# Layer 3's two sets of scans in one sequence with weights set up beside the end of layer 2, images moved in thirds, and GpSimd side steps in the sixth group

## The chip, the core and the metric

The program runs on one core of a Trainium2 chip, as one launch. Its engines work side by side and meet at semaphores: TensorE (PE), VectorE (DVE), ScalarE (ACT), GpSimd (POOL) and SyncE (SP, which here only issues DMA transfers). The metric is the time on the device from the first to the last instruction, in microseconds; lower is better.

## The reference

Four images of 48 x 48 positions with 192 channels pass through four layers, all in fp32. The core of each is a selective scan with 16 states a channel, over the 2,304 positions of an image or over each of its 48 rows or columns:

```python
def step(h, t):                      # one position of a sequence
    d_t, u_t, b_t, c_t = t
    h = exp(d_t[..., None] * A) * h + (d_t * u_t)[..., None] * b_t[:, None, :]
    return h, sum(h * c_t[:, None, :], -1)
# layer 0: _mamba = in_proj, causal conv, silu, scan, gate silu(z), out_proj
xw = _mamba(columns) + _mamba(columns reversed)
xh = layernorm(xw as rows) + x;  x = _mamba(xh) + _mamba(xh reversed)
# layer 1: convolutions on half of the channels; on the other half
yv = the scan in 4 directions (rows, columns, both reversed), added up
x = shuffle(concat(conv half, out_proj(layernorm(yv) * silu(z)))) + x
# layer 2: the scan in 4 directions once more, added up
x = layernorm(y)
# layer 3
xn = layernorm(x)
h = _mamba of each row of xn, forward and reversed, concatenated    # set "mh"
v = _mamba of each column of xn, forward and reversed, concatenated # set "mv"
x = x + fc(concat(v, h)) + fc_b
x = x + mlp(layernorm(x))
```

Row-order and column-order versions of the images are both kept in DRAM, since a scan reads its sequence in order.

## The kernel before

**Stages.** Layer 0 is two calls of `mamba_pair`. `vss_inputs` does the convolutions of layer 1. `scan_layers` does the scans of layers 1 and 2 for all four images in one sequence. Layer 3 is `row_mambas` twice, first for the set "mv" on the column-order images `xn_wh`, then for "mh" on `xn_hw`; then `mlp`.

**Jobs and groups.** A *job* is a chunk of 384 positions (6 to an image) in one direction. `run_jobs` runs a list of jobs group by group. A *group* covers 128 partitions of channels and four of the states: VectorE multiplies `du` by the broadcast row B (`inputs`, line 56), scans (`h`), GpSimd multiplies h by the broadcast row C (`h<-h,bcb`), TensorE adds up over the states (`y`), and ACT computes the four exponentials `a` two groups ahead. A job has 6 groups in layers 1 and 2 and 12 in layer 3. The work that prepares the next job (`units`: loads of `u` or `xs`, projections, the convolution, the products for B, C and delta) and that ends the last one (`outputs`) is spread over the groups, at numbered *slots*; slot 0 is a job's first group. What VectorE, GpSimd, TensorE in most of its products, and ACT issue is kept in program order (class `InOrder`, line 48). DMA transfers of SP aren't: they are issued when their inputs and buffers are ready.

**The ends of layers 1 and 2.** When the fourth direction of an image has been scanned, the sum of its directions is normalised and projected, in six chunks of 384 columns, last first. `vss_end` and `ss2d_end` give a list of *steps* for a chunk, each with a kind: "dma" (loads), "act", "pe" (a product into PSUM and its copy by ACT), "both", "pool" (the norm's scale, `nx<-nx,nrs` on GpSimd). `Side` (line 689) puts at most one step into each group, in the slots of the step's kind. What is left after the last scan, which is part of the third image of layer 2 and the fourth image whole, is done by `Side.finish`, with new buffers and all of PSUM.

**Images in column order.** For each image the end of a layer needs the sum of the column directions in row order and gives its result in both orders. At the first chunk (`c == NCH - 1`), `load` loads a whole image, 1.7 MB, into `turned`; each chunk's `turn` copies its part of it (`no<-turned`), and later its results are copied back into the same place (`turned<-no`); after the last chunk (`c == 0`), `turned` is stored whole as `x_wh` or `xn_wh`.

**Layer 3.** `row_mambas` opens its pools, loads the set's weights, multiplies the output projection by the matching part of fc (`fp`), builds its `ScanPools`, and runs its 48 jobs. The second call does so again after the first has run empty. The results f of both sets stay in DRAM apart. `mlp` loads its weights, then at each image's start (`pre`) the residual x3 and both results, adds them up in `macc` by four VectorE passes, one half of the channels each, and goes on chunk by chunk: norm, first product, Gelu, second product.

Of the kernel before, what the change touches and what calls it, by code (L numbers as in the profile page):

```python
# [291 lines left out]


# [395 lines left out]
class Side:  # L689
# [4 lines left out]
    slots = {"pe": (0, 4, 5), "both": (0, 4), "act": (0, 4, 5), "pool": (0, 2, 4), "dma": range(6)}  # L694
# [25 lines left out]
    def finish(self):  # L720

        while self.waiting:
            n = len(self.waiting) if self.waiting[0][0][0] == "dma" else 1
            some, self.waiting = self.waiting[:n], self.waiting[n:]
            for steps in zip(*some):
                for step in steps:
                    self.begin(*step)
                    self.end()


def run_jobs(jobs, side=None):
# [14 lines left out]
    def offer(job):  # L746
        if side is not None and job.steps is not None:
            side.waiting.append(job.steps())
# [12 lines left out]
    for t in range(len(groups) + gated):  # L761
        n, at = divmod(t, per)
        if at == 0:
            last = jobs[n - 1] if n else None
            if n + 1 < len(jobs):
                jobs[n + 1].load()
                stream = Stream(jobs[n + 1].units(last))
        if at == per - ahead:
            stream.run(at - 1)
        if at == taken + 3 and n + 1 == len(jobs) and n:  # L770
            Stream(jobs[n - 1].outputs(*[(0, 0)] * 4)).run(per)
        if t < len(groups):
            job, i, g = groups[t]
            job.scan(i, g)
        coming = at_group(t + 1, 0)
        if t + ahead < len(groups):
            job, i, g = groups[t + ahead]
            job.decay(i, g, (lambda: coming[0].enter(coming[1])) if coming else None)
        if done := at_group(t - taken, last_group):
            done[0].take(done[1])  # L780
        if t < len(groups):
            if t + 1 < len(groups):
                job, i, g = groups[t + 1]
                job.carry(i, g)
            job, i, g = groups[t]
            job.weigh(i, g)
        stream.run(at if at < per - 1 else per)
        if side is not None and t < len(groups):
            if at == taken + 1 and n:
                offer(jobs[n - 1])  # L790
            side.slot(at)
            side.end()
        if done := at_group(t - gated, last_group):
            done[0].gate(done[1])
        if begun := at_group(t + driven, 0):
            begun[0].drive(begun[1])
        if 0 <= t - behind < len(groups):
            job, i, g = groups[t - behind]
            job.reduce(i, g)
# [38 lines left out]
class MambaWeights(Weights):  # L838
    def __init__(self, k, pool, inT, xpT, dtT, vec, tag):
        super().__init__(k, pool, 128, 12, xpT, dtT, vec, tag)  # L840
        self.decays(k)
        nc = k.nc
        self.D = self.vec[:, :, 17:18]
# [7 lines left out]
        self.inT = k.tile(pool, [Q, 2, 768], f"inT{tag}")  # L851
        nc.sync.dma_start(self.inT, inT.rearrange("(k p) m -> p k m", p=Q))
        self.diag = k.tile(pool, [128, 3, self.taps, 128], f"diag{tag}")
        for i in range(3):
            for t in range(self.taps):
                nc.vector.tensor_scalar(
                    self.diag[:, i, t, :],
                    k.ident,
                    self.vec[:, i, 19 + t : 20 + t],
                    None,  # L860
                    ALU.mult,
                )

# [20 lines left out]
def mamba_pair(k, weights, srcs, first, outs, ahead=None):  # L884


    with ExitStack() as ctx:
# [3 lines left out]
        def load():  # L891
            for n, (inT, xpT, dtT, vec, outT) in enumerate(weights):
                w = MambaWeights(k, pool, inT, xpT, dtT, vec, f"_{n}")
                w.outT = k.tile(pool, [128, 3, C], f"outT_{n}")
# [239 lines left out]
class Normed:  # L1134
# [17 lines left out]

    def tile(self, shape, tag, bufs=None):
# [7 lines left out]
    def rows(self, turned, c):  # L1161

        t = self.tile([Q, 2, CH], "no")
        for m in range(2):
            self.k.copy(
                t[:, m, :].rearrange("p (r l) -> p r l", l=S), rows_of(turned[:, m, :], c)
# [49 lines left out]

def rows_of(img, c):
# [28 lines left out]
def scan_layers(k, pool, layers, ends):  # L1246
# [3 lines left out]
    with ExitStack() as ctx:  # L1250
        one = ctx.enter_context(k.tc.tile_pool(name="s1", bufs=1))
        two = ctx.enter_context(k.tc.tile_pool(name="s2", bufs=2))
# [33 lines left out]
        scans.close()  # L1286
        normed.two = ctx.enter_context(k.tc.tile_pool(name="s3", bufs=NCH))
        side.psum = ctx.enter_context(k.tc.tile_pool(name="sp", bufs=8, space=PSUM))
# [3 lines left out]
def vss_end(k, vec, outT, x1, xl, zs, out_hw, out_wh):  # L1292
# [3 lines left out]
    def begin(normed, one):  # L1296
# [5 lines left out]
        turned = {}  # L1302

        def steps(b, c, h_sum, w_sum):
# [3 lines left out]
            def load():  # L1308
                if c == NCH - 1:
                    turned[b] = k.tile(normed.one, [Q, 2, L], "turned")  # L1310
                    nc.sync.dma_start(turned[b], halves(w_sum))
# [8 lines left out]
            def turn():  # L1320
                st["w"] = normed.rows(turned[b], c)
# [14 lines left out]
            def result(s):  # L1336
# [6 lines left out]
                def act(ps):  # L1343
# [3 lines left out]
                    k.copy(rows_of(turned[b][:, s, :], c), ps.rearrange("p (r l) -> p r l", l=S))  # L1347
                    if s == 1:
                        parts = "(c s) l -> c s l"
                        nc.sync.dma_start(out_hw[b].rearrange(parts, s=2)[:, :, at], st["o"])  # L1350
                        if c == 0:
                            nc.sync.dma_start(out_wh[b].rearrange(parts, s=2), turned[b])
# [3 lines left out]
            return [  # L1356
# [6 lines left out]
            ]  # L1363

# [5 lines left out]
def ss2d_end(k, vec, ln1, x3, xn_hw, xn_wh):  # L1370
# [3 lines left out]
    def begin(normed, one):  # L1374
# [4 lines left out]
        turned = {}  # L1379

        def steps(b, c, h_sum, w_sum):
# [3 lines left out]
            def load():  # L1385
                if c == NCH - 1:
                    turned[b] = k.tile(normed.one, [Q, 2, L], "turned")
                    nc.sync.dma_start(turned[b], halves(w_sum))
                st["y"] = normed.load("ny", halves(h_sum)[:, :, at])

            def turn():
                st["w"] = normed.rows(turned[b], c)
# [10 lines left out]
            def second(x, of):  # L1403
                o = normed.tile([Q, 2, CH], "no")
                for m in range(2):
                    of(o[:, m, :], m)
                    k.copy(
                        rows_of(turned[b][:, m, :], c),
                        o[:, m, :].rearrange("p (r l) -> p r l", l=S),
                    )  # L1410
                nc.sync.dma_start(halves(xn_hw[b])[:, :, at], o)
                if c == 0:
                    nc.sync.dma_start(halves(xn_wh[b]), turned[b])

            return [
# [6 lines left out]
            ]  # L1422

# [5 lines left out]
def row_mambas(k, weights, fcT, srcs, outs):  # L1429


    with ExitStack() as ctx:
        pool = ctx.enter_context(k.tc.tile_pool(name="w", bufs=1))
        inT, xpT, dtT, vec, wout = weights
        w = MambaWeights(k, pool, inT, xpT, dtT, vec, "")
        ws = [w, copy(w)]
        wo = k.tile(pool, [Q, 2, 2 * C], "wo")
        k.nc.sync.dma_start(wo, wout.rearrange("(k p) m -> p k m", p=Q))
        fc = k.tile(pool, [Q, 2, 2, C], "fc")
        for n in range(2):  # L1440
            k.nc.sync.dma_start(fc[:, n, :, :], fcT[n].rearrange("(k p) m -> p k m", p=Q))

        outT = [k.tile(pool, [128, 3, C], f"outT_{n}") for n in range(2)]
        with k.tc.tile_pool(name="fp", bufs=2, space=PSUM) as fp:
            for n in range(2):
                for i in range(3):
                    p = k.tile(fp, [128, C], "fp")
                    k.mm(p, [(wo[:, m, i * 128 : (i + 1) * 128], fc[:, n, m, :]) for m in range(2)])
                    k.copy(outT[n][:, i, :], p)
        pools = ScanPools(k, ctx, 1, True)  # L1450
        jobs = []
        for n in range(2):
            ws[n].outT = outT[n]
        for b in range(B):
            for c in range(NCH):
                of = None, srcs[b], outs[b]
                first = MambaJob(k, pools, ws[0], c * CH, False, *of)
                jobs += [first, MambaJob(k, pools, ws[1], c * CH, True, *of, twin=first)]
# [3 lines left out]
def mlp(k, f, fcb, ln2, w1T, b1, w2T, b2, x3, out):  # L1462
# [5 lines left out]
    with (  # L1468
# [5 lines left out]
    ):  # L1474
        w1 = k.tile(one, [Q, 2, 3 * C], "mw1")
# [9 lines left out]
        nw = k.tile(one, [Q, 2, 3], "mnw")  # L1485
        nc.sync.dma_start(nw[:, :, 0:2], ln2.rearrange("(k p) v -> p k v", p=Q))
        nc.sync.dma_start(nw[:, :, 2:3], fcb.rearrange("(k p v) -> p k v", p=Q, v=1))
        acc, xn, hid = {}, {}, {}

        def pre(b):  # L1490
            acc[b] = k.tile(pool, [Q, 2, L], "macc")
            nc.sync.dma_start(acc[b], halves(x3[b]))
            y = []
            for n in (1, 0):
                y.append(k.tile(one, [Q, 2, L], f"mf{n}"))
                nc.sync.dma_start(y[-1], halves(f[n][b]))
            for m in range(2):
                nc.vector.scalar_tensor_tensor(
                    acc[b][:, m, :], acc[b][:, m, :], nw[:, m, 2:3], y[0][:, m, :], ALU.add, ALU.add
                )  # L1500
            for m in range(2):
                nc.vector.tensor_tensor(
                    square(acc[b][:, m, :]),
                    square(acc[b][:, m, :]),
                    flipped(y[1][:, m, :]),
                    ALU.add,
                )
# [33 lines left out]
def network(tc, d, out):  # L1541
    with ExitStack() as ctx:
# [23 lines left out]

        xl, zs = images("xl", Q), images("zs")
# [4 lines left out]
        with tc.tile_pool(name="w", bufs=1) as pool:  # L1572
            weights = []

            def beside(b):
# [19 lines left out]
                ],  # L1595
            )
# [3 lines left out]
        for n, (p, src) in enumerate((("mv", xn[1]), ("mh", xn[0]))):  # L1600
            ws = tuple(d[f"L3_{p}_{v}"] for v in ("inT", "xpT", "dtT", "vec", "Wout"))
            fcT = [d["L3_fcT"][2 * n + i] for i in range(2)]
            row_mambas(k, ws, fcT, src, f[n])
        mlp(k, f, *(d[f"L3_{v}"] for v in ("fc_b", "ln2", "w1T", "b1", "w2T", "b2")), x3, out)


# [115 lines left out]
```

## Time and profile before

| | |
|---|---|
| Median of three runs | 20,027.88 us (20,027.85 to 20,035.81) |
| Profiled execution | 20,028.4 us |
| TensorE, VectorE, GpSimd, ACT busy | 88%, 91%, 73%, 64% |
| Layer 0, first pair and second pair, from first to last scan | 44.5 to 3,131 and 3,331 to 6,419 us |
| `vss_inputs` | 6,422 to 6,925 us |
| `scan_layers`, scans | 6,925.2 to 13,205.4 us (1,152 groups) |
| "mv" and "mh", scans | 13,386.6 to 16,440.0 and 16,503.7 to 19,553.2 us (576 groups each) |
| `mlp` | to 20,028.4 us |

The stages are read from the starts of the scan instruction (`h<-a,inputs`) in the timeline of VectorE. In the profile's list of groups, a line gives the source line, the engine, the operation, output and inputs by the names of the program, their shape, and after x the count; then the total busy time and the mean of one in ns; then the idle time of the engine just ahead of them and what ended most of it. Line 56 is that of the in-order helper and line 93 that of ACT's, so the names tell such operations apart. A line of the waits says which engine and which operation waited for what, then the total time, the number of waits, and the longest. A line of the timeline has start, duration, engine and operation, and in brackets the idle time ahead and its releaser.

### The profile page before, as it was taken

What the parts mean: (1) busy time and instruction counts of PE and PEld (TensorE: products, weight loads), DVE (VectorE), ACT (ScalarE), POOL (GpSimd) and SP (SyncE); (2) the same over time, 40 slices, a digit from 0 to 9 for tenths busy, and PEclk for the clock granted to TensorE, in tenths of its full rate; (3) what the DMA queues carried; (4) which work ended last, traced back from release to release, by engine and by line L of the source; (5) the groups of instructions that cost most, each with busy time, mean ns of one, the idle gap of its engine ahead of it and who ended that gap; (6) DMA issues with size and microseconds to landing.
All of it is one profiled execution on the core that took longest, in us unless ns stands there. A gap on an engine that the chain in (4) does not pass through costs nothing.

```text
span 20028.4 us, 159197 instructions
## 1 busy us (share of the span) xinstructions
PE 17551.3 (88%) x48144; PEld 8281.4 (41%) x48144; DVE 18198.7 (91%) x7435; ACT 12796.7 (64%) x22447; POOL 14681.9 (73%) x10816
## 2 busy tenths in 40 slices
PE   8999997999998878888888888879989989999988
PEld 4444443444444322333333332334444444444444
DVE  8999997999998499999999999969999989999993
ACT  6666665666665466666666766666666656666663
POOL 7888885788786177887877877857777767777770
PEclk9999998999999889999999999989999999999999
DMA  3333333333233366666666666642222222222322
GB/s 116 108 109 110 115 110 111 109 113 115 103 110 100 82 133 138 142 146 146 143 147 143 138 139 144 138 110 103 101 106 104 106 96 106 107 101 102 107 102 59
DMA packets 484426, 2313.40 MB, mean 116 GB/s; under 512 B 75401, under 2 KB 324017, under 8 KB 325553
## 3 DMA queue, kind: packets, MB, share of 16 engines
q1 hardware_dynamic: 483568, 2303.21, 40.7%
q8 instruction: 386, 6.32, 0.1%
q14 instruction: 472, 3.86, 0.1%
HBM read 2110.68 MB, written 192.32 MB: 115 GB/s over the span
## 4 chain that ended last, share of the span: by engine, by line
DVE 35%; POOL 13%; PE 10%; issue 5%; ACT 2%; DMA 2%; DVEq 0%; SPq 0%; POOLq 0%; ACTq 0%
DVE h L56 23%; DVE inputs L56 12%; POOL h L56 10%; PE y L56 5%; PE ps L56 3%; POOL dus L56 1%; PE vps L114 1%; ACT a L93 1%; PE mop L114 1%; PE mps L114 1%; DMA bcb<-bc 1%; POOL state L56 1%; DVE vxi L1056 1%; DVEq L56 0%; POOL bcb L56 0%
## 5 line engine op out<-in xcount | busy, mean ns | idle before, releaser
L56 POOL TENSOR_TENSOR h<-h,bcb 128x1536 f32<-128x1536 f32 x3456 | 11914.0, 3447 | 1764.2 <-DVE h L56 1489.3
L56 DVE TENSOR_TENSOR_SCAN h<-a,inputs 128x1540 f32<-128x1540 f32 (+1 forms) x3456 | 11609.8, 3359 | 449.2 <-ACT a L93 10.8
L93 ACT ACTIVATE a<-delta,A 128x384 f32<-128x384 f32 (+1 forms) x13824 | 7431.8, 602 | 3417.4 <-DVE h L56 3405.2
L56 PE MATMUL y<-h,ident 128*128 128x384 f32 x18432 | 6798.4, 517 | 587.2 <-POOL h L56 581.9
L56 DVE TENSOR_TENSOR inputs<-du,bcb 128x1540 f32<-128x1540 f32 (+1 forms) x3456 | 6115.4, 1770 | 561.0 <-ACT du L93 205.9
L56 PEld LDWEIGHTS y<-h,ident 128*128 128x128 f32 x18432 | 3619.4, 201 | 3625.1 <-POOL h L56 1100.6
L56 PE MATMUL y<-h,sum 128*64 128x384 f32 x9216 | 3666.4, 547 | 598.3 <-POOL h L56 486.6
L56 PEld LDWEIGHTS y<-h,sum 128*64 128x64 f32 x9216 | 1294.8, 150 | 2922.0 <-issue 1755.0
L56 POOL COPY state<-h 128x4 f32<-128x4 f32 x2304 | 434.0, 188 | 2296.2 <-DVE h L56 2277.1
L56 PE MATMUL ps<-xh,diag 128*128 128x384 f32 x4032 | 1417.3, 491 | 196.3 <-ACT xc L93 196.3
L56 PE MATMUL ps<-u,inT 96*128 96x384 f32 x3456 | 1263.1, 497 | 189.9 <-ACT z L93 135.4
L56 PE MATMUL ps<-bcd,dtT 12*128 12x384 f32 (+1 forms) x2304 | 1019.4, 550 | 388.9 <-ACT delta L93 384.7
L56 PEld LDWEIGHTS ps<-xh,diag 128*128 128x128 f32 x4032 | 750.4, 189 | 790.0 <-ACT xc L93 283.0
L93 ACT ACT_TABLE_LOAD x793 | 1017.4, 1283 | 14.2
L90 ACT ACT_TABLE_LOAD x784 | 1005.9, 1283 | 14.3 <-PEq L1712 0.7
L56 PEld LDWEIGHTS ps<-u,inT 96*128 96x128 f32 x3456 | 652.2, 192 | 704.1 <-ACT z L93 213.0
L93 ACT ACTIVATE delta<-ps,vec 128x384 f32<-128x384 f32 x1152 | 632.5, 579 | 324.0 <-PE ps L56 316.9
L56 PE MATMUL ps<-yt,outT 128*96 128x384 f32 x2304 | 789.5, 486 | 0.7 <-POOL yt L56 0.7
L56 PEld LDWEIGHTS ps<-bcd,dtT 12*128 12x128 f32 (+1 forms) x2304 | 382.5, 192 | 958.1 <-ACT delta L93 622.0
L56 POOL TENSOR_TENSOR dus<-delta,xc 128x384 f32<-128x384 f32 x576 | 575.4, 999 | 130.8 <-ACT delta L93 130.8
L93 ACT ACTIVATE du<-dus 128x384 f32<-128x384 f32 x1152 | 558.2, 485 | 160.5 <-DVE inputs L56 155.0
L93 ACT ACTIVATE o<-ps 96x384 f32<-96x384 f32 x288 | 140.3, 487 | 716.6 <-PE ps L56 716.6
(131 smaller groups left out, 9694.9 us busy)
## 6 DMA issues: line engine op xcount, KB each, us to landing
bcb<-bc SPq DMA_DIRECT2D x384, 1540.0 KB
bcb<-bc SPq DMA_DIRECT2D x768, 770.0 KB
bcb<-bc SPq DMA_DIRECT2D x384, 1536.0 KB
y<-o SPq DMA_DIRECT2D x192, 288.0 KB
xs<-xi_wh SPq DMA_DIRECT2D x96, 288.0 KB
xs<-xi_hw SPq DMA_DIRECT2D x96, 288.0 KB
added<-y SPq DMA_DIRECT2D x96, 288.0 KB
xs<-x_wh SPq DMA_DIRECT2D x96, 288.0 KB
```

What stands on the lines that cost most here:

```text
L56: return lambda *a, **kw: self.tc.keep_in_program_order(op(*a, **kw))
L90: self.in_order(self.nc.scalar.preload_act_table_set(LOG_EXP))
L93: return self.in_order(self.nc.scalar.activation(out, in_, func, **kw))
L114: (engine or self.nc.tensor).matmul(out, lhsT, rhs, start=start and i == 0, stop=stop and i == n - 1)
L1056: nc.vector.scalar_tensor_tensor(acc, taps, v[:, i, 1 + t : 2 + t], acc, ALU.mult, ALU.add)
```

## The change

`row_mambas` gets both sets and runs them as one list of 96 jobs. A new class `RowWeights` sets up both sets' weights; it is called (`ahead`) inside `scan_layers`, after the steps already begun and before the rest of `Side.finish`. The second set's `inT` takes the place of the first's, and is loaded by a job's `extras`. The second set adds x3 as its `prior`, so that `mlp` no longer loads it. `Normed.image` puts three DMA steps ahead of an image's first chunk and three after its last, in place of the whole transfers, and `turned` is one tile for all images. "pool" steps may also go into slot 5. After the scans, one of a chunk's two copies into `turned` is VectorE's (`flip`). `mlp` loads its inputs by halves and ahead, and adds them up in one VectorE pass for each half.

```diff
-    slots = {"pe": (0, 4, 5), "both": (0, 4), "act": (0, 4, 5), "pool": (0, 2, 4), "dma": range(6)}
+    slots = {"pe": (0, 4, 5), "both": (0, 4), "act": (0, 4, 5), "pool": (0, 2, 4, 5), "dma": range(6)}
...
-    def finish(self):
+    def finish(self, begun=False):
         while self.waiting:
-            n = len(self.waiting) if self.waiting[0][0][0] == "dma" else 1
+            new = [steps[0][0] == "dma" != steps[-1][0] for steps in self.waiting]
+            n = max(1, [*new, False].index(False))
+            if begun and new[0]:
+                break
...
         if side is not None and job.steps is not None:
-            side.waiting.append(job.steps())
+            side.waiting += job.steps()
...
         stream.run(at if at < per - 1 else per)
+        if t < len(groups):
+            for slot, extra in jobs[n].extras:
+                if slot == at:
+                    extra()
...
+    def enter(self, tag="inT"):
+        self.inT = self.k.tile(self.pool, [Q, 2, 768], tag)
+        self.k.nc.sync.dma_start(self.inT, self.in_src.rearrange("(k p) m -> p k m", p=Q))
...
+    def image(self, c, src, steps, dst):
+        def move(out, in_):
+            return lambda: self.k.nc.sync.dma_start(out, in_)
+        def parts(out, in_):
+            n = L // 3
+            at = [slice(i * n, (i + 1) * n) for i in range(3)]
+            return [[("dma", move(out[:, :, a], in_[:, :, a])) for a in at]]
+        ahead = parts(self.turned, src) if c == NCH - 1 else []
+        return [*ahead, steps, *(parts(dst, self.turned) if c == 0 else [])]
+    def flip(self, m, dst, src):
+        if m == 1 and self.alone:
+            self.k.nc.vector.tensor_copy(dst, src)
+        else:
+            self.k.copy(dst, src)
...
         scans.close()
+        normed.alone = True
+        side.psum = ctx.enter_context(k.tc.tile_pool(name="sp", bufs=6, space=PSUM))
+        side.finish(True)
+        beside.close()
         normed.two = ctx.enter_context(k.tc.tile_pool(name="s3", bufs=NCH))
-        side.psum = ctx.enter_context(k.tc.tile_pool(name="sp", bufs=8, space=PSUM))
+        ahead()
         side.finish()
...
-                if c == NCH - 1:
-                    turned[b] = k.tile(normed.one, [Q, 2, L], "turned")
-                    nc.sync.dma_start(turned[b], halves(w_sum))
                 st["y"] = normed.load("ny", halves(h_sum)[:, :, at])
...
-                if c == 0:
-                    nc.sync.dma_start(halves(xn_wh[b]), turned[b])
...
+            return normed.image(c, halves(w_sum), steps, halves(xn_wh[b]))
...
+class RowWeights:
+    def __init__(self, k, pool, raw, psum, sets):
+        self.pairs = []
+        for s, (ws, _) in enumerate(sets):
+            w = MambaWeights(k, pool, *ws[:4], f"_{s}")
+            self.pairs.append((w, copy(w)))
+        self.pairs[0][0].enter()
+        for s, (ws, fcT) in enumerate(sets):
+            wo = k.tile(raw, [Q, 2, 2 * C], "wo", 1)
+            k.nc.sync.dma_start(wo, ws[4].rearrange("(k p) m -> p k m", p=Q))
+            fc = k.tile(raw, [Q, 2, 2, C], "fc", 1)
+            for n in range(2):
+                k.nc.sync.dma_start(fc[:, n, :, :], fcT[n].rearrange("(k p) m -> p k m", p=Q))
+            for n in range(2):
+                w = self.pairs[s][n]
+                w.outT = k.tile(pool, [128, 3, C], f"outT_{s}{n}")
+                for i in range(3):
+                    p = k.tile(psum, [128, C], "fp")
+                    at = slice(i * 128, (i + 1) * 128)
+                    k.mm(p, [(wo[:, m, at], fc[:, n, m, :]) for m in range(2)])
+                    k.copy(w.outT[:, i, :], p)
...
+        for (there, back), (srcs, outs, prior) in zip(weights.pairs, sets):
+            if jobs:
+                jobs[-2].extras = [(1, there.enter)]
+            for b in range(B):
+                for c in range(NCH):
+                    of = None, srcs[b], outs[b]
+                    last = prior[b] if prior is not None else None
+                    first = MambaJob(k, pools, there, c * CH, False, *of)
+                    jobs += [
+                        first,
+                        MambaJob(k, pools, back, c * CH, True, *of, twin=first, prior=last),
+                    ]
         run_jobs(jobs)
...
+        def load(b):
+            acc[b] = k.tile(pool, [Q, 2, L], "macc")
+            y = k.tile(pool, [Q, 2, L], "mf")
+            for m in range(2):
+                nc.sync.dma_start(y[:, m, :], f[0][b][m * Q : (m + 1) * Q, :])
+                nc.sync.dma_start(acc[b][:, m, :], f[1][b][m * Q : (m + 1) * Q, :])
+                nc.vector.scalar_tensor_tensor(
+                    square(acc[b][:, m, :]),
+                    square(acc[b][:, m, :]),
+                    nw[:, m, 2:3],
+                    flipped(y[:, m, :]),
+                    ALU.add,
+                    ALU.add,
+                )
+        load(0)
...
         def pre(b):
-            acc[b] = k.tile(pool, [Q, 2, L], "macc")
-            nc.sync.dma_start(acc[b], halves(x3[b]))
-            y = []
-            for n in (1, 0):
-                y.append(k.tile(one, [Q, 2, L], f"mf{n}"))
-                nc.sync.dma_start(y[-1], halves(f[n][b]))
...
+            if b + 1 < B:
+                load(b + 1)
...
-            row_mambas(k, ws, fcT, src, f[n])
+        row_mambas(k, made[0], [(xn[1], f[0], None), (xn[0], f[1], x3)])
+        rows.close()
```

## The prediction

> **What bounds the kernel now.** I read the page's shares first, then its costliest groups, the waits of VectorE, and then the timeline at each place where a wait of VectorE is long.
>
> ```profile
> PE 17551.3 (88%) x48144; PEld 8281.4 (41%) x48144; DVE 18198.7 (91%) x7435; ACT 12796.7 (64%) x22447; POOL 14681.9 (73%) x10816
> ...
> L56 POOL TENSOR_TENSOR h<-h,bcb 128x1536 f32<-128x1536 f32 x3456 | 11914.0, 3447 | 1764.2 <-DVE h L56 1489.3
> L56 DVE TENSOR_TENSOR_SCAN h<-a,inputs 128x1540 f32<-128x1540 f32 (+1 forms) x3456 | 11609.8, 3359 | 449.2 <-ACT a L93 10.8
> ...
> L56 DVE TENSOR_TENSOR inputs<-du,bcb 128x1540 f32<-128x1540 f32 (+1 forms) x3456 | 6115.4, 1770 | 561.0 <-ACT du L93 205.9
> ```
>
> A group of the scan is one VectorE multiply (1.77 us), one scan (3.36) and one GpSimd multiply (3.45). The 3,456 groups keep VectorE busy for 17,725 of 20,028 us, and they follow each other at a median of 5.37 us in the scans of layers 1 and 2 and 5.29 in those of layer 3 (starts of scans in the timeline). The change leaves these instructions alone. So it can win only in the holes between groups:
>
> ```profile
> DVE inputs L56 <- ACT du L93: 205.9, 38, 35.0
> DVE ones L249 <- DMA u<-xn_wh: 135.2, 1, 135.2
> ...
> DVE macc L1498 <- DMA mf<-f: 43.0, 1, 43.0
> DVE ones L249 <- DMA f<-o: 17.7, 1, 17.7
> ```
>
> Each of the last three is one hole at a stage's border. The starts of the scans around them, and the mlp's first two passes, in the timeline of VectorE:
>
> ```profile
> 13205.37 3.36 DVE L56 TENSOR_TENSOR_SCAN h<-a,inputs 128x1540 f32<-128x1540 f32 x1
> ...
> 13386.58 3.35 DVE L56 TENSOR_TENSOR_SCAN h<-a,inputs 128x1536 f32<-128x1536 f32 x1 [1.70 <-ACT a L93]
> ...
> 16439.98 3.35 DVE L56 TENSOR_TENSOR_SCAN h<-a,inputs 128x1536 f32<-128x1536 f32 x1
> 16503.65 3.35 DVE L56 TENSOR_TENSOR_SCAN h<-a,inputs 128x1536 f32<-128x1536 f32 x1 [1.71 <-ACT a L93]
> ...
> 19599.54 5.14 DVE L1498 SCALAR_TENSOR_TENSOR macc<-macc,mnw,mf 96x2304 f32<-96x2304 f32 x2 [42.98 <-DMA mf<-f]
> ```
>
> Layer 2 to layer 3: 177.9 us without a scan. Between the two sets of layer 3: 63.7 from scan to scan, 58.4 over a group. Inside layers 1 and 2 the groups' mean is 5.456, so 1,151 intervals hold 100.5 us above the median; six places of 8.8 to 13.7 us, one for each image whose end is formed beside the scans, make up 65 of it. The first of them:
>
> ```profile
> 8508.82 0.53 SPq L1352 DMA_DIRECT2D x_wh<-turned  x1
> 8509.44 3.22 SPq L463 DMA_DIRECT2D xs<-xi_hw  x2
> 8518.68 0.32 SPq L1311 DMA_DIRECT2D turned<-y  x1
> ```
> ```profile
> 8538.77 1.77 DVE L56 TENSOR_TENSOR inputs<-du,bcb 128x1540 f32<-128x1540 f32 x1 [8.80 <-ACT du L93]
> ```
>
> The 1.7 MB store of an image in column order is queued 0.6 us ahead of the next job's xs. TensorE's xs product then stands 6.3 us for that load (to 8521.4), ACT's copy behind it 8.2 for the product, and du comes 8.8 late. In layer 2, ACT's copy out of `turned` also stands 13.9 to 14.2 us for the load of the image, and every exponential and du is queued behind it.
>
> **What the Trainium skill says.** "DMA: Bandwidth & Descriptors", section "Queues, rings and completion order": on each DMA engine, descriptors are consumed in the order of the ring. The trace agrees: xs waits behind the big store. "Perfetto Trace Analysis", "Optimization Strategy": a kernel with several regimes can gain by interleaving them. Here the regimes are the scans and the ends of layers, and the holes above are where they aren't interleaved.
>
> **The change part by part.** Sums are made against the profiled span of 20,028.4; the three runs lie at 20,027.9 to 20,035.8, so no shift is needed.
>
> *One sequence in layer 3.* The border goes: its drain, the second set's weights, its products and its first u. The second set's inT (0.6 MB) is loaded during the next-to-last job of the first set, 12 groups of 5.29 = 63 us long, in a stage where DMA moves some 105 of over 200 GB/s. I take −58.4: 63.7 becomes 5.3. Bounds: −40, if the load into the single inT buffer makes the first u of the second set late; −58.4 is all there is. The second set's `prior` costs two GpSimd adds a pair of jobs: the existing add of this shape takes 996 ns. They sit in groups 7 and 8, which have no dus or yt; GpSimd has 5.29 − 3.45 − 0.5 = 1.3 us free there. I take 0, at most 48 × 0.3 = 14.
>
> *Images in thirds.* A third is 0.58 MB. A whole image took 10.5 us with its landing, so a third takes about 3.5, and one is issued per group of 5.37 us. By counting the steps into slots, the "in" thirds come ahead of an image's first chunk and the "out" thirds after its last, in jobs whose xs is already there. xs then waits at most 3.5 us, inside the 3 to 4 groups for which it is loaded ahead. In slots 3 to 5 of each job, though, the queue is busy throughout with the job's own loads (213 GB/s). I take 65 down to 3.5; bounds 0 and 15. So −61.5.
>
> *GpSimd steps in the sixth group.* The steps are the norm's scale, 994 ns each, 40-odd that land in slot 5 by count. Odd groups already carry dus, also 1.0 us:
>
> ```profile
> 8121.94 3.45 POOL L56 TENSOR_TENSOR h<-h,bcb 128x1536 f32<-128x1536 f32 x1
> 8125.35 1.00 POOL L56 TENSOR_TENSOR dus<-delta,xs 128x384 f32<-128x384 f32 x1
> 8126.29 0.20 POOL L56 COPY bcb<-state 128x4 f32<-128x4 f32 x1
> 8127.10 0.19 POOL L56 COPY state<-h 128x4 f32<-128x4 f32 x1 [0.61 <-DVE h L56]
> 8127.36 3.45 POOL L56 TENSOR_TENSOR h<-h,bcb 128x1536 f32<-128x1536 f32 x1
> ```
>
> GpSimd is idle 0.6 us in such a group, so a step of effective 0.94 pushes the next state copies, and the `inputs` behind bcb, by 0.4: 39 × 0.4 = +16. Bounds: 0, if VectorE's slack of a group absorbs it; 39, if all of each step shows. (The skill, "GPSIMD Engine Reference", 3.1, gives 4,497 ns for a two-input add of 2,048 elements, which scales to an estimate of 843 for 384; the trace's 994 is used.) In return, a chunk of 12 steps goes through in fewer groups, so the four steps of the third image that ran on after the scans now fit into them.
>
> *The end of layer 2.* Counted from the end of the last scan, T0 = 13,208.7. Before: the leftover steps and the store of xn_wh, then the load of the last image landing at +36.2; the six chunks' end to +125.5, ACT copying; the xn_wh store to about +135; weights, their products, u, first scan at +177.9. After: the weights' space comes free at about +6.6; 14 loads of 0.47 = 6.6, landing 4.8, products and copies 6.4; the second set's wo and fc share one buffer, so again 1.4 + 4.8 + 6.4, and the last copy 0.6. ACT runs in program order, so its first `turn` of the chunks comes at +37.6 instead of +36.2. The chunks took 89.4; six ACT flips of 0.86 go to VectorE (a row of 384 fp32 there is 0.25 to 0.5 us, an estimate from "VectorE: DVE Perf Modes", "The perf-mode tier table", 1,227 ns at 2,048; no VectorE copy of this shape is in the trace), where they lie beside ACT: 84.7. Then the last third of the store, about 12 with its landing and u's load, and 27.5 from u to the first scan as before. Sum 161.8, so −16. Bounds: +5, if the weights hold ACT longer; −45, if only the first set's weights stand in the way.
>
> *mlp.* Before, x3 and two sets of f are loaded behind the weights (macc waits 43.0) and four VectorE passes follow. After: f's store lands, 2.7 us to release, two 0.5 us loads, halves of 1.7 MB landing at +14 and +23, one pass of 4.1 after each; the first ln_xm comes some 16 us earlier, at about 29 us instead of 45.7 after the last f store. At the next three borders TensorE waits 7.8 us in all for macc; I take 4. So −20, bounds −8 and −26. The rest of this stage is TensorE's (97% busy), and nothing there changes.
>
> Sum: −58.4 − 61.5 + 16 − 16 − 20 = −139.9; 20,028.4 becomes **19,888**.
>
> **The rivals.** (1) The weights hold up the end of layer 2: the transition gains 0 or loses 5, and 19,905 to 19,912 comes out. For it: ACT is in order, and single wo and fc buffers make two landings in a row. Against: 36 us of idle ACT are there in any case. Its opposite, `turn` at +12, would give 19,863. (2) Thirds don't help: SP issues when a transfer's inputs allow, and the three may go out at once and again ahead of xs. The 65 stay: 19,950. For it: in this trace an image's load was issued 230 us before its slot; against: `turned` is now one tile that the copies of the chunk before still read. (3) Slower: GpSimd in the sixth group. If each of 42 steps delays `inputs` by more than (140 + 16)/42 = 3.7 us, all gains are gone; from 4.7 us each it is slower by over 0.2% (40 us, about what a measurement of this kernel tells from no change), above 20,068. It would need a step to cost a whole group, by bringing ACT's or TensorE's order with it; a 1 us step beside 0.6 us of idle speaks against. (4) The join is not seamless, since inT's single buffer waits for the first set's last use: half of 58 comes back, 19,917 to 19,945. That the sets aren't joined at all is excluded by the diff.
>
> **How the numbers follow.** Forecast 0.70, (1) 0.12 with its opposite in the range, (2) 0.10, (3) 0.02, (4) 0.06. The forecast's own bounds: all good ends together give 19,834, all bad ones 19,988; they won't fall together, so 19,840 to 19,950, which also takes in (1), (4) and (2)'s centre. Faster by over 0.2% means under 19,988: 0.95; within 0.2%: 0.03; slower: 0.02.
>
> **What would show it.** Right: one scan distance of about 5.3 at the join, no VectorE wait for u<-xn_hw; no hole of 8 us or over behind `du` in layers 1 and 2, the mean distance there down from 5.456 to about 5.41; first scan of layer 3 some 160 us after T0; the first macc pass about 25 us after f's store. Wrong: GpSimd's added time in slot 5 shown as `inputs` <- bcb waits of over 0.4 us each; ACT's first `turned` copy at over T0 + 40; a wait for xs at the images' places; or the groups' medians of 5.37 and 5.29 moved, which no step here foresees and which would outweigh all of them: 0.1 us on a median over 1,152 groups is 115 us.

## The result, and the profile after

The changed kernel takes 19,872.54 us (median of four runs, 19,865.94 to 19,882.17) beside 20,031.85 for the kernel before on the same chip: a ratio of 0.992, 95% interval 0.9903 to 0.9937, so 159 us less. The forecast was 19,888 in a range from 19,840 to 19,950. The profiled executions differ by 164.3 us (20,028.4 and 19,864.1). From the starts of the scans, that difference falls on four stages:

| Stage | before | after | difference | forecast |
|---|---|---|---|---|
| scans of layers 1 and 2, first to last | 6,280.2 | 6,217.6 | −62.6 | −61.5 + 16 |
| last scan of layer 2 to first of layer 3 | 181.2 | 160.0 | −21.2 | −16 |
| scans of layer 3, both sets and the border | 6,166.6 | 6,104.2 | −62.4 | −58.4 |
| last scan of layer 3 to the end | 475.2 | 457.5 | −17.7 | −20 |

The waits of VectorE over the whole run, after (what waited for what, total, number, longest):

```profile
DVE turned L1192 <- ACT no L93: 93.9, 6, 86.9
...
DVE inputs L56 <- ACT du L93: 68.3, 16, 28.5
...
DVE macc L1547 <- DMA macc<-f: 44.8, 4, 29.2
...
DVE inputs L56 <- POOL bcb L56: 28.8, 46, 3.2
```

The wait of `inputs` for du fell from 205.9 us in 38 places to 68.3 in 16; inside the scans of layers 1 and 2 alone, it fell from 82.1 in 34 to 13.1 in 14. The wait of 135.2 for u<-xn_wh has another name now: VectorE's first instruction after the scans is the flip of an image's half (line 1192), and it stands 86.9 us for ACT. A wait that changes its name hasn't become shorter; only the starts of the scans tell. The waits for bcb, the mark of GpSimd's steps in slot 5, rose from 14.6 us in 11 places to 28.8 in 46. The timeline of VectorE at the borders:

```profile
13142.51 3.36 DVE L56 TENSOR_TENSOR_SCAN h<-a,inputs 128x1540 f32<-128x1540 f32 x1
...
13302.47 3.35 DVE L56 TENSOR_TENSOR_SCAN h<-a,inputs 128x1536 f32<-128x1536 f32 x1 [1.01 <-ACT a L93]
...
16351.86 3.35 DVE L56 TENSOR_TENSOR_SCAN h<-a,inputs 128x1536 f32<-128x1536 f32 x1
16357.21 3.35 DVE L56 TENSOR_TENSOR_SCAN h<-a,inputs 128x1536 f32<-128x1536 f32 x1
...
19439.21 4.12 DVE L1547 SCALAR_TENSOR_TENSOR macc<-macc,mnw,mf 96x2304 f32<-96x2304 f32 x1 [29.18 <-DMA macc<-f]
```

16,351.86 is the last scan of the set "mv", 16,357.21 the first of "mh": 5.35 us where 63.7 were. The last line is mlp's first addition. In layers 1 and 2 no distance between scans is more than 2.1 us over the median of 5.369, where six places of 8.7 to 13.7 us had been, each of one to three distances (the prediction's 8.8 is VectorE's wait at the first).

### The profile page after: what moved, and what is told of

Same layout as the page of the kernel before. It is cut to its first block, busy times and chain, and to the rows that moved or that the text cites. A ratio compares the mean times of both kernels' runs of the same rounds, so it can differ in the third digit from the quotient of the medians.

```text
span 19864.1 us, 159334 instructions
## 1 busy us (share of the span) xinstructions
PE 17521.5 (88%) x48144; PEld 8275.2 (42%) x48144; DVE 18181.7 (92%) x7432; ACT 12794.6 (64%) x22443; POOL 14712.9 (74%) x10864
## 5 line engine op out<-in xcount | busy, mean ns | idle before, releaser
L56 DVE TENSOR_TENSOR inputs<-du,bcb 128x1540 f32<-128x1540 f32 (+1 forms) x3456 | 6114.9, 1769 | 460.4 <-ACT du L93 68.3
```

The costliest lines, as they stand in the source:

```text
L56: return lambda *a, **kw: self.tc.keep_in_program_order(op(*a, **kw))
```

## The experiments

They ran on three chips, on which the kernel before takes 20,028.6 to 20,037.3 us, so a difference of a run's time to the 19,872.54 of the change is good to some 10 us; the stages of the profiles are the finer measure. "The way to layer 3" is the time from the start of the last scan of layer 2 to that of the first scan of layer 3.

**GpSimd back to three slots.**

```diff
-    slots = {... "pool": (0, 2, 4, 5), "dma": range(6)}
+    slots = {... "pool": (0, 2, 4), "dma": range(6)}
```

> GpSimd steps back to slots 0, 2 and 4, all else as in the change. My theory: the sixth slot costs about 0.3 us for each of its 42 steps in the scans of layers 1 and 2 (-13 here), but without it a chunk with the thirds no longer fits: by counting, two chunks and the out thirds of the third image are left over after the last scan, which adds some 60 us between layer 2 and layer 3. Time 35 to 60 us above the change, 19,905 to 19,930. Rival A: the steps in slot 5 cost as much as they bring, so within 10 us of the change. Rival B: they only cost, and this is 10 us or more faster than the change.

Measured: 19,979.13 us, ratio to the kernel before 0.9974 (0.9965 to 0.9984); 107 above the change, far over what was expected. The way to layer 3 took 218.3 us, 58 more, as counted. The surprise is in the scans: not 13 us less but 46 more (6,263.6). The images move in thirds here as well, and yet VectorE's holes are back, nine distances of scans 3.6 to 5.3 us over the median. Each of the first three images has two of them. Here are both for the first image, from the timelines of SP, GpSimd, TensorE and VectorE:

```profile
8558.59 1.91 SPq L360 DMA_DIRECT2D bcb<-bc  x2
...
8571.60 1.26 SPq L466 DMA_DIRECT2D xs<-xi_hw  x2
```
```profile
8579.87 0.19 POOL L56 COPY bcb<-state 128x4 f32<-128x4 f32 x1 [4.97 <-DMA bcb<-bc]
```
```profile
8570.72 0.80 PE L56 MATMUL y<-xs,ddiag 64*64 64x384 f32 x2
...
8583.57 4.06 PE L56 MATMUL ps<-xs,xpT 64*38 64x384 f32 x6 [6.74 <-DMA xs<-xi_hw]
```
```profile
8580.09 1.77 DVE L56 TENSOR_TENSOR inputs<-du,bcb 128x1540 f32<-128x1540 f32 x1 [4.53 <-POOL bcb L56]
...
8601.16 1.77 DVE L56 TENSOR_TENSOR inputs<-du,bcb 128x1540 f32<-128x1540 f32 x1 [5.07 <-ACT du L93]
```

All six thirds, three out and three in, were issued here within 18 us (8,542.7 to 8,560.6). The first hole comes from the broadcast rows of B and C (`bcb`), whose loads stand between the thirds. The second comes from xs, which was wanted 5.2 us after its issue and landed after 12. So thirds by themselves keep neither load from waiting.

**Whole images in the same places.**

```diff
-            return [[("dma", move(out[:, :, a], in_[:, :, a])) for a in at]]
+            return [[("dma", move(out, in_))]]
```

> The image in column order moves in one DMA step each way instead of three, in the same places of the step lists. The prediction's theory (the size of a third is what keeps xs, bcb and the copies from waiting): VectorE's holes of 8 us or over behind du come back at six images, 40 to 65 us above the change, about 19,915 to 19,935. Rival (it is the place of the move, ahead of the first chunk and a slot or more behind the last, and not its size): no hole of over 4 us, at most 10 us above the change.

Measured: 19,893.82 us, 21 above the change; the scans 6,246.2 (+28.6), the rest as in the change. This lies between the two expectations: no hole is over 3.2 us (the rival allowed 4), but there are 49 waits for du of 50.1 us in all, where the change has 14 of 13.1. These holes aren't the moves'. At the longest, and in the same way at the next two, ACT stands for a product of the side steps' norm on TensorE, and du is queued behind it:

```profile
9363.60 0.49 ACT L93 ACTIVATE nx<-ps 96x384 f32<-96x384 f32 x1 [8.38 <-PE ps L56]
```
```profile
9366.44 1.77 DVE L56 TENSOR_TENSOR inputs<-du,bcb 128x1540 f32<-128x1540 f32 x1 [3.19 <-ACT du L93]
```

An image has four steps fewer here, so the steps behind them fall into other groups. No product of TensorE waits for xs in this run. The 28.6 us are therefore not shown to be the price of large transfers.

**The kernel before with the sixth slot alone.** The first experiment's edit the other way round, in the kernel before.

> The kernel before with one edit: GpSimd steps may go into slot 5 too. Images still move whole, ahead of and behind their first and last chunk. My theory now: the sixth slot makes chunks shorter, so that an image's moves fall some five jobs earlier, into a pass of the first column direction, in which TensorE is 80% busy and not 93% and no sum of the earlier directions is loaded; the holes of 8.8 to 13.7 us vanish (no hole over 4 us), the 42 steps in slot 5 cost 13 us, and the last image is loaded before the scans end. Scans of layers 1 and 2 about 35 us shorter, the way to layer 3 10 to 25 us shorter: 19,965 to 19,985. Rival (the size of the moves made the holes): the holes stay and the slot only costs, 20,028 to 20,042.

Measured: 19,955.88 us, ratio 0.9961 (0.9946 to 0.9976), 78 us below the kernel before, somewhat better than expected. The scans take 6,236.1 us (−44.1), the way to layer 3 150.7 (−30.5); the border in layer 3 (63.6) and mlp are as before. No hole is over 2.4 us, though every image moves in one piece. The theory of the place holds. What waited for transfers inside the scans of layers 1 and 2, in us:

| | before | first experiment | slot alone | whole images | the change |
|---|---|---|---|---|---|
| TensorE's products, for xs | 48.9 | 34.9 | none | none | none |
| ACT, for the image in `turned` | 28.1 | 3.7 | 2.2 | 0.8 | none |
| GpSimd, for the rows of bcb | 15.7 | 51.1 | 19.8 | 3.4 | 15.5 |

The first row comes from these lines of the waits, of the kernel before and of the first experiment:

```profile
PE ps L56 <- DMA xs<-x_hw: 28.5, 3, 11.1
PE ps L56 <- DMA xs<-xi_hw: 20.4, 3, 7.1
```
```profile
PE ps L56 <- DMA xs<-x_hw: 20.7, 4, 7.5
PE ps L56 <- DMA xs<-xi_hw: 14.2, 2, 7.5
```

The timelines show the place. SP and TensorE in the change, in a pass of the first column direction:

```profile
8362.18 1.24 SPq L1179 DMA_DIRECT2D x_wh<-turned  x2
8363.52 5.08 SPq L360 DMA_DIRECT2D bcb<-bc  x4
8368.71 1.27 SPq L466 DMA_DIRECT2D xs<-xi_wh  x2
```
```profile
8387.70 2.12 PE L56 MATMUL ps<-xs,xpT 64*38 64x384 f32 x6
```

Here xs is issued 19 us ahead of its use, behind two thirds that go out back to back, and nobody waits. In the pass of the last direction, where the moves of the kernel before and of the first experiment fell, the lead was 5 to 6 us. The code says why: there, the chunk of xs is also added to the output at each block of channels (`skip` with `diag`), so that its buffer comes free later. In the first experiment's lines above, the last of these additions (`y<-xs,ddiag`) ends at 8,571.5, and xs is issued at 8,571.6. The same pass is TensorE's fullest (busy time of TensorE first, in the pass with the moves and in the one after it, of the change):

```profile
8284.60:8478.30 193.70, 152.20 (x384) 53.45 (x382) 184.81 (x73) 125.51 (x228) 155.95 (x134) 0.91 0.70 154
8478.30:8674.10 195.80, 177.11 (x469) 63.22 (x469) 184.78 (x73) 130.03 (x236) 156.01 (x134) 0.93 0.65 142
```

TensorE is 79% and 90% busy there. Which of the two matters more, the lead of xs or TensorE's slack, was not separated.

**A second GpSimd step in slot 5.**

```diff
+            if at == 5 and self.waiting[0][0][0] == "pool":
+                self.k.g.tensor_tensor(self.scratch, self.scratch, self.scratch, ALU.mult)
             self.begin(*self.waiting[0].pop(0))
...
```

> The change, with one more GpSimd multiply of 96x384 (on a scratch tile, its result isn't used) ahead of each of the 42 steps in slot 5. My theory: GpSimd has 0.6 us free in such a group, the first step uses it up and delays the next group by 0.3, a second delays by its whole effective 0.94: +39 us, 19,912. Rival: what a group loses is made up by the next even group, which has 1.5 us free, so the second costs no more than the first, +0 to +13 us. Rival that could have made the change slower: over 3.7 us for each step, +155 us.

Measured: 19,904.94 us, 32 above the change; the scans +35.4, or 0.84 us for each of the 42 steps. VectorE's waits for bcb inside the scans, of the change and then with the second step:

```profile
DVE inputs L56 <- POOL bcb L56: 24.0, 44, 1.4
```
```profile
DVE inputs L56 <- POOL bcb L56: 50.4, 46, 1.9
```

Nothing is made up later. In the change, the groups behind such a step are 5.694 us apart in the mean and the others at that place 5.395: 0.30 for each, 12.6 us in all. By the same distances the second step shows 0.64 of its 0.84, so the full cost of the first may be somewhat above 0.30.

**Two sequences in layer 3, weights early.**

```diff
-        jobs = []
-        for (there, back), (srcs, outs, prior) in zip(weights.pairs, sets):
-            if jobs:
-                jobs[-2].extras = [(1, there.enter)]
+        for n, ((there, back), (srcs, outs, prior)) in enumerate(zip(weights.pairs, sets)):
+            jobs = []
+            if n:
+                there.enter()
...
-        run_jobs(jobs)
+            run_jobs(jobs)
```

> The two sets of layer 3 as two sequences of 48 jobs, one run after the other on the same pools, with both sets' weights set up early as in the change. The border before was 63.7 us from scan to scan: 17.5 to empty the pipeline, 17 for weights and their products, 28 to fill it. My theory: emptying and filling come back, the weights don't: 45 us from scan to scan, 41 above the change, about 19,913. Rival: the weights were what mattered, and the border is under 25 us. Second rival: all of it comes back (63 us), because inT of the second set is loaded only then.

Measured: 19,913.15 us, 41 above the change, as expected. VectorE's timeline at the border:

```profile
16356.55 3.35 DVE L56 TENSOR_TENSOR_SCAN h<-a,inputs 128x1536 f32<-128x1536 f32 x1
16403.07 3.35 DVE L56 TENSOR_TENSOR_SCAN h<-a,inputs 128x1536 f32<-128x1536 f32 x1 [1.71 <-ACT a L93]
```

46.5 us: of the 58.4 that the join saves, 41 are emptying and filling the pipeline and the other 17 are what the early weights save.

**Weights behind the end of layer 2.**

```diff
-        ahead()
         side.finish()
+        ahead()
```

> The set-up of layer 3's weights (ahead) is put after the rest of the end of layer 2 in program order, instead of before it; its transfers may still go early, but ACT's copies of the products come behind the six chunks. My theory (ACT's order holds the chunks' first turned copy at 32 us after the last scan, where the image is there at about 10): the chunks start 20 to 24 us earlier, the weights' copies fit into the wait for the store of xn_wh, so 15 to 22 us below the change, about 19,853. Rival: the products and copies land on the path between the chunks and the first scan, and the time is within 8 us of the change or above it.

Measured: 19,859.47 us, 13 below the change, which the times alone hardly tell from none. The way to layer 3 does: it takes 146.5 us here and 145.1 in another run with this order (below), and 159.9 to 166.1 in the six profiles with four slots and the weights early. ACT's timeline, in the change and with this edit:

```profile
13177.83 0.33 ACT L93 ACTIVATE outT<-fp 128x192 f32<-128x192 f32 x1 [0.36 <-PE fp L114]
13178.07 9.05 ACT L93 ACTIVATE no<-turned 96x384 f32<-96x384 f32 x12
```
```profile
13156.42 9.03 ACT L93 ACTIVATE no<-turned 96x384 f32<-96x384 f32 x12 [3.50 <-DMA vec<-in_L_mv_vec]
```

The chunks start 21.6 us earlier. Of these, 8 are given back. The chunks now take 88.1 us instead of 82.5: TensorE, which had its first products of them 0.4 us before ACT's first copy in the change, starts 3.4 us after it, and it begins slowly. TensorE with this edit:

```profile
13159.84 2.84 PE L56 MATMUL ps<-ny,center 96*96 96x384 f32 x4 [4.64 <-ACT no L93]
...
13166.87 1.45 PE L56 MATMUL ps<-no,center 96*96 96x384 f32 x4
```

The other 2.5 come after the chunks, where, by the code, the second set's wo still waits for the buffer of the first.

**mlp's loads late.**

```diff
-        load(0)
...
-            if b + 1 < B:
-                load(b + 1)
+            load(b)
```

> In mlp, an image's inputs are loaded at its own start (the first image's behind the weights of mlp, as before), all else as in the change. My theory: the first norm comes about 6 us later, since 12 issues of 0.5 us stand ahead of its loads, and each of the three borders between images loses 1 to 2 us: 8 to 12 us above the change, about 19,882. Rival: transfers go when their buffers are free whatever the program's order, so that it is within 3 us of the change.

Measured: 19,877.95 us, 5 above the change, which the times can't tell from none. The trace can in one place: from the last store of f to the first norm it takes 32.4 us, in the change 26.6 (before: 45.7). The borders between images show nothing.

**Towards a better version.** Three steps, each on top of the one before. First, weights behind the end, two buffers for wo and fc, and a second share for VectorE once the scans are over:

```diff
-            self.k.copy(square_rows(t[:, m, :]), rows_of(turned[:, m, :], c))
+            self.flip(m, square_rows(t[:, m, :]), rows_of(turned[:, m, :], c))
...
+            if m == 1 and self.alone:
+                k.nc.vector.tensor_scalar(dst, x, gm, bm, ALU.mult, ALU.add)
```

> The change with the weights' set-up behind the end of layer 2, two buffers for wo and fc, and after the scans VectorE taking the second half of the copies out of the image and of the norm's last scaling, beside the flip that it has. Expected against the change: the 13.5 us of the run with the set-up behind, 3.5 for the second set's wo and fc no longer waiting for the first's products, 4.5 for the copies out, 3.7 for the first scaling and some 3 for the second, where GpSimd's steps bound: 25 to 30 us in all, about 19,845, with the first scan of layer 3 about 130 us after the last one of layer 2. Rival: TensorE or GpSimd sets the pace of the chunks, and only the 13.5 and 3.5 are to be had: 19,855.

Measured: 19,864.95 us, the way to layer 3 145.1: the share and the second buffers together took off 1.3 us of the 146.5, and the rival was right that VectorE's share gives nothing. ACT's timeline in the change says so beforehand; from the sixth on, every pair of copies out of the first norm's products stands for TensorE, as in:

```profile
13193.55 0.49 ACT L93 ACTIVATE nx<-ps 96x384 f32<-96x384 f32 x1 [1.72 <-PE ps L56]
```

So the second step takes work off TensorE:

```diff
+            self.k.nc.vector.tensor_tensor(
+                square_rows(y[:, m, :]), square_rows(y[:, m, :]),
+                rows_of(turned[:, m, :], c), ALU.add,
+            )
...
```

> The kernel of the run before (weights behind the end of layer 2, VectorE's share after the scans), and after the scans VectorE adds the two sums of directions while it takes the column-order one out of the image, so that TensorE centres one source instead of two. My theory, from the run before, where taking work off ACT moved nothing: TensorE sets the pace of the first norm, 48 products of 0.645 us; 24 of them go (-15.5), and the 12 additions of about 0.5 us take the place of the copies. First scan of layer 3 about 130 us after the last one of layer 2 instead of 145, the time 12 to 18 us lower, about 19,850. Rival: the chunks wait for GpSimd's scaling and the chain of the norm, and the distance stays over 140.

Measured: 19,849.76 us; the way to layer 3 131.4, and the same wait of ACT is 0.43 where it was 1.72: TensorE did set the pace. Third, the first image of mlp by chunks:

```diff
+            if b == 0:
+                for m in range(2):
+                    nc.sync.dma_start(y[:, m, :], f[0][b][m * Q : (m + 1) * Q, :])
+                for c in range(NCH):
+                    at = slice(c * CH, (c + 1) * CH)
+                    nc.sync.dma_start(acc[b][:, :, at], halves(f[1][b])[:, :, at])
...
```

> The run with the sum first, and in mlp the first image's residual and second result are loaded and added up chunk by chunk behind the whole of the first result, instead of by halves. My theory: the first norm needs 2 MB instead of 3.5 and two short passes instead of two of 4.1 us: 10 to 14 us earlier, so 19,838 beside 19,850 of the run with the sum first. Rival: the loads are slowed by their number, or TensorE has to wait for the later chunks' passes: within 4 us.

Measured: 19,843.23 us, ratio to the kernel before 0.9903 (0.9888 to 0.9917); from the store of f to the first norm 20.3 us, and 25.8 without this step: 5.5 us, between the expected 10 to 14 and the rival's 4. The changed kernel itself, beside these two:

> The changed kernel once more, unedited, beside the two runs above: 19,866 to 19,882 as in its four runs.

Measured: 19,874.98 us. The last version is 32 us below it. This run also shows how far one profile can be trusted: with the same code, the way to layer 3 is 165.2 us where it was 160.0, and mlp 461.3 where it was 457.5, while the two stages of scans agree to 0.4.

## Why the prediction was right, and where its reason wasn't

**The join: right.** Forecast −58.4; at the border 63.7 became 5.35. No wait for u<-xn_hw appears, and the prior's additions show nowhere. The remaining 4 us of the stage are not the join's (last section).

**The sixth slot's cost: right.** Forecast +16 from 0.4 us a step; measured +12.6 from 0.30 in the distances right behind the steps. The rival that would have ended slower needed 3.7 us a step. A doubled step gave 0.84, so that rival was far off.

**The images: the cause wrong, the size partly luck.** Forecast −61.5; the scans' −62.6 with the slot's 12.6 taken out leave −75. That is outside the forecast's own bound, since the six places held 65; the other 10 lie in smaller waits between them and were not traced. The step that failed is the booking of the gain: "xs then waits at most 3.5 us, inside the 3 to 4 groups for which it is loaded ahead" puts it down to the size of a third and gives the slot a cost of 16. The lead was read rightly from the count of steps (19 us, 3.6 groups), but it comes from the slot. With three slots, thirds make holes of 5 us; with four, whole images make none of over 3.2, and the slot alone takes 44.1 of the 62.6 us. The change had both, so the sum came out near the forecast although its cause didn't hold. The sums of the scans and the way to layer 3 by what is there:

| | three slots | four slots |
|---|---|---|
| whole images | 6,461.4 (before) | 6,386.8 (slot alone) |
| thirds | 6,481.9 (first experiment) | 6,377.6 (the change) |

The rows differ in more than the thirds: the upper row has no weights set up early and no flips of VectorE. With these, and whole images as a step of their own, the four slots give 6,406.1. So what the thirds are worth is not shown: without the slot the lower row is 20 us longer, which fits the six steps that they add to an image, and with it 9 shorter. The sixth slot, booked in the prediction as a cost of 16 with four leftover steps in return, is what moves the transfers into a pass where xs has a long lead and TensorE more slack. It also keeps two chunks from being left over, which is worth 58 us on the way to layer 3 once there are thirds. Rival (2) was half right as well: two of three thirds do go out at once. They do no harm where they fall.

**The end of layer 2: size right, one term wrong.** Forecast −16, measured −21.2. The first copy out of the image came at +32.2 instead of +37.6, the chunks took 82.5 instead of 84.7 (six flips of 0.86 off 89.4 would be 84.2), from their end to u 14 instead of 12, and the rest 27.9, about as counted. But what was booked as the gain of early weights isn't one: rival (1) named the mechanism, ACT's order, and moving them behind takes another 13 us off, while the kernel before with the slot alone, its weights loaded last, needs only 150.7. So the gain is rather that of the leftover steps and of the last image's store and load, 36 us of the stretch before, much of which the slot lets happen beside the scans. The slot alone gives 30.5: its chunks end 95.3 us after the last scan instead of 125.5.

**VectorE's flips** took 0.48 to 0.72 us, where the prediction's estimate, scaled from the 1,227 ns for 2,048 elements in the Trainium skill, "VectorE: DVE Perf Modes", section "The perf-mode tier table", was 0.25 to 0.5. Three of the six fit it, and the longest is 0.72; ACT's took 0.85.

**mlp: right.** Forecast −20; −17.7, and −19.2 at its beginning alone (45.7 to 26.6 us). The 4 us at the borders between images were not found.

## What to carry to other kernels

A side step on an engine with a little idle time (0.6 us of a group here) is priced by what it delays, but it is worth what its place in the sequence lets others reach: here some 0.3 us a step bought a shorter chain of steps, and with it the transfers' move into a pass where the next load has 19 us of lead instead of 5. Before cutting a transfer into pieces, measure how far ahead of its use each load behind it is issued. In these runs xs was waited for where that lead was 5 to 6 us, behind thirds as behind a whole image, and not where it was 19 or more; how much TensorE's slack had to do with it stays open. And set-up work that is copied by an engine working in program order, as ACT does here, belongs behind the critical chain, even if its loads can go early.

## What the runs showed of the hardware that was not expected

The scans of layer 3 took 6,104 to 6,105 us in the change and in three of its variants, and 6,111 to 6,112 in five others whose loops are the same. Single groups make the difference: some 20 of 1,152, 30 to 92 groups apart, are each 0.35 to 0.44 us longer, and at most two in the faster builds; in VectorE's timeline of the run with the weights last, the scan waits for the multiply just ahead of it on its own engine:

```profile
15985.96 3.35 DVE L56 TENSOR_TENSOR_SCAN h<-a,inputs 128x1536 f32<-128x1536 f32 x1 [0.48 <-DVE inputs L56]
```

The first set of the kernel before has the same 0.4 us steps and loses 4 us by them, which are the rest of the −62.4. What causes them stays open; a few microseconds in a comparison of two builds can be this.
